# A three-layer graph network on one core: pieces of up to 104 edges in five units, other list lengths, distances on ScalarE, leaky relu on GpSimd

## The chip, the core and the metric

The kernel runs on one core of a Trainium2 chip. The metric is the device time of one execution in microseconds. Its engines work side by side, each through its own queue in order: TensorE (PE in the profile, its weight loads PEld), VectorE (DVE), ScalarE (ACT), GpSimd (POOL) and SyncE (SP, here only for starting transfers). Gathers by an index are started by GpSimd.

## The reference, cut to what matters

```python
def _sage_conv(x, src, dst, Wl, bl, Wr):
    agg = jax.ops.segment_max(x[src], dst, num_segments=x.shape[0])
    agg = jnp.where(jnp.isfinite(agg), agg, 0.0)
    return agg @ Wl + bl + x @ Wr

h = jnp.maximum(_layernorm(x, axis=-1), 0.0)
h = leaky_relu(_sage_conv(h, src, dst, Wl1, bl1, Wr1), 0.01)
h = leaky_relu(_sage_conv(h, src, dst, Wl2, bl2, Wr2), 0.01)
h = leaky_relu(_sage_conv(h, src, dst, Wl3, bl3, Wr3), 0.01)
return x + h
```

There are 6250 nodes and 200000 edges, sorted by destination; the first nodes have by far the most edges. The widths are 128, 256, 256 and 128.

## The kernel before

The nodes are cut into 50 tiles of 127 (the last one shorter). For each destination the maximum over its sources is taken in two ways. For each pair of source tiles g (25 pairs), a product of the rows of that pair with a one-hot matrix picks one source row per destination column, and VectorE takes the maximum into an accumulator. Edges that find their place taken go into lists, whose rows GpSimd gathers from the table of node values, and VectorE takes their maximum too.

Destination tiles are "units" in five groups. Narrow units (24 and 4) have one column per pair of source tiles; middle (11) and wide units (8) have one for each source tile. The three heaviest tiles (`VT`) are cut into pieces of up to `CUT_V` = 96 edges; the pieces fill `NV` = 6 virtual units of 128 rows, and each of these has two columns per source tile: the unit itself and its extra ("x") unit for the second edge. So that group has 12 units in `PLANES`, in parts of 8 and 4. `Joined` puts the pieces of a node together again.

A step is one part of one pair's columns: 8 units in layer 0, up to 4 in layers 1 and 2, so 225, 375 and 375 steps. `products` (L1002) does the matrix products of a step, `maxima` (L1026) the maxima, once for the narrow units and once for each of the two source tiles for the others. One-hots are made by ScalarE (L983, L985) from index bytes, up to six buffers ahead.

The order is written out: `plan(t, rank, f)` enters work for step t, and the main loop runs the ranks of a step in a fixed order (list indices, transposes of h, half of the products, maxima of lists and "chores", rows, rest, linear, merge, gathers, fetches, the other half of the products).

- The lists: `CAPS` gives the length of the list for each block of 128 rows (rows are sorted by length), `PACK` that of one group of rows which are longer still. `Listed.gather` (L1064) gathers one row for each of 128 destinations and writes zeros into a scratch tile after it, 300 columns, as a pause (L1068). `Listed.maximum` (L1079, L1084) follows 4 to 8 steps later. The gathers of a layer are spread over its steps. Eight tiles of gathered rows exist. The index tile of each gather is made by ScalarE (L1053).
- The chores: work on the edge lists that is still to be done during layer 0. `late_rows` sorts and sends lists, `late_lookups` finds for each group of units, in batches of five pairs, which edge belongs to which pair: `expand` (L772) computes the distance of each edge's code to the pair's code by an exclusive or, halves the row by minima (L778) and reduces it (L779); `lookups` transposes the result on TensorE and ScalarE copies it out (L806). The code of a source is its tile times 128, plus its place, plus one, and the lowest bits of the exclusive or are the place if tile and pair agree.
- The nodes: `Node` finishes one tile. Fetch at step ta, merge at ta + 3, `linear` (L1147, L1149; ScalarE copies z to s, L1151) at ta + 4, `rows` at ta + 5 (VectorE's leaky relu into h, L1158, or L1162 in the last layer, and the store of h), `turn` at ta + 6 (TensorE transposes h, L908; ScalarE copies the transpose and h rounded to the product's type, L910 and L913), `rest` in the same step (VectorE's remainder of the rounding, L918, and its store). Nodes come one per step in layer 0 and for the wide units, and one in two steps otherwise in layers 1 and 2.

If a list or a tile does not fit its limits, a flag sends the run through a general path, which redoes all by loops over single edge columns.

## Time and profile before

| | us |
|---|---|
| median of 3 runs (3161.16 to 3170.59) | 3166.22 |
| the profiled execution | 3162.05 |
| its span | 3160.2 |
| VectorE busy | 2717.8 (86%) |
| GpSimd busy | 2430.8 (77%) |
| TensorE busy | 2332.1 (74%) |
| ScalarE busy | 1433.9 (45%) |

Busy shares are means over stretches with different limits. The stretches used further on were found by counting the products of L1002 in program order: layer 0 begins at 229 us, layer 1 at 1216 us, layer 2 at 2201 us, and the span ends at 3160 us. From 397 to 538 us the look-ups of the virtual units are among the chores; from 665 to 825 us the first 24 nodes of layer 0 are finished, one per step; from 1116 to 1284 us the other nodes of layer 0. From 1284 to 1836 us and from 2270 to 2820 us layers 1 and 2 have products and lists alone; from 1836 and from 2820 us on nodes are finished beside them.

### The profile page before, as it was taken

How to read it: one execution, taken by the hardware profiler on the slowest of the kernel's cores; microseconds unless marked ns; L12 is line 12 of the kernel's file. 1: busy time of each engine (PE TensorE's matmuls, PEld its weight loads, DVE VectorE, ACT ScalarE, POOL GpSimd, SP SyncE). 2: the span in 40 equal slices, each digit the busy share in tenths (PEclk: the TensorE clock that was granted, in tenths of full speed). 3: DMA queues.
4: the chain of work that ended last, by engine and by line, in shares of the span. 5: the costliest groups of instructions: out<-in, count | busy, mean ns of one | idle time of the engine just before them, and what ended most of it. 6: DMA issues, size and time to landing. Idle time of an engine off the chain costs nothing.

```text
span 3160.2 us, 37328 instructions
## 1 busy us (share of the span) xinstructions
PE 2332.1 (74%) x9394; PEld 1710.8 (54%) x9394; DVE 2717.8 (86%) x4441; ACT 1433.9 (45%) x2394; POOL 2430.8 (77%) x3424
## 2 busy tenths in 40 slices
PE   1024554456566778899888878889999988888997
PEld 1023333334344455677666656666676666666665
DVE  6668988987898975999999988876799999998995
ACT  5214443333544666555454434444555545443342
POOL 6666888688778883888888786763688888788882
PEclk9996766777767999999999999999999999999998
DMA  9322334266645797556454456778455554555675
GB/s 259 116 65 82 116 111 115 80 179 215 197 156 174 221 270 243 160 157 189 144 153 151 149 162 217 235 217 265 155 172 162 174 141 156 157 153 174 201 221 153
DMA packets 303458, 538.58 MB, mean 170 GB/s; under 512 B 57245, under 2 KB 165589, under 8 KB 302595
## 3 DMA queue, kind: packets, MB, share of 16 engines
q1 hardware_dynamic: 206573, 302.97, 29.7%
q0 software_dynamic: 78592, 196.07, 23.0%
q10 hardware_dynamic: 18070, 37.07, 3.1%
q8 instruction: 79, 1.29, 0.2%
q14 instruction: 144, 1.18, 0.1%
HBM read 409.84 MB, written 126.04 MB: 170 GB/s over the span
## 4 chain that ended last, share of the span: by engine, by line
DVE 19%; PE 16%; POOL 12%; DMA 6%; issue 6%; ACT 1%; SPq 0%; DVEq 0%; POOLq 0%; ACTq 0%
DVE acc L1026 13%; PE pg L1002 11%; POOL g L1064 8%; DMA g<-table,let 4%; POOL gap_t L1068 3%; DVE g L1079 2%; DVE g L1084 2%; PE z_p L1147 2%; PE z_p L1149 1%; DMA out_dram<-s 1%; DMA pair_sb<-pair 1%; ACT hot L985 0%; DMA agg_v<-best,end_i 0%; PE hT_p L908 0%; DMA xt<-in_x_dram 0%
## 5 line engine op out<-in xcount | busy, mean ns | idle before, releaser
L1002 PE MATMUL pg<-hot,pair_sb 128*128 128x512 f32 (+1 forms) x7500 | 2036.3, 421 | 414.2 <-DVE acc L1026 241.3
L1002 PEld LDWEIGHTS pg<-hot,pair_sb 128*128 128x128 f32 x7500 | 1436.1, 202 | 873.4 <-issue 285.9
L1064 POOL DMA_INDIRECT g<-table,let x1518 | 1523.9, 1004 | 492.6 <-issue 237.6
L1026 DVE TENSOR_TENSOR acc<-acc,pg 128x1024 f32<-128x1024 f32 (+4 forms) x1614 | 1663.6, 1057 | 207.1 <-PE pg L1002 164.7
L985 ACT ACTIVATE hot<-idx_sb 128x1024 fp32r<-128x1024 uint8 (+2 forms) x1050 | 909.6, 886 | 714.0 <-PE pg L1002 548.5
L1068 POOL MEMSET gap_t<- 128x300 f32 x1518 | 566.5, 373 | 0.7
L983 ACT ACTIVATE hot<-idx_sb,last_b 128x1024 fp32r<-128x1024 int8 (+1 forms) x300 | 310.3, 1034 | 37.2 <-PE pg L1002 24.9
L1118 POOL DMA_INDIRECT agg<-best,end_i x141 | 140.1, 994 | 104.1 <-PE aT_p L1134 60.5
L1151 ACT COPY s<-z_p 127x256 f32<-127x256 f32 (+1 forms) x150 | 50.4, 336 | 363.2 <-PE z_p L1149 325.8
L1079 DVE TENSOR_TENSOR g<-g 128x1024 f32<-128x1024 f32 (+6 forms) x214 | 207.8, 971 | 0.3
L1084 DVE TENSOR_TENSOR g<-g 128x256 f32<-128x256 f32 (+3 forms) x377 | 183.2, 487 | 11.2 <-issue 0.2
L1147 PE MATMUL z_p<-wr,hT_in 128*128 128x256 f32 (+1 forms) x500 | 138.7, 395 | 0.6 <-DMA hT_in<-across 0.6
L1149 PE MATMUL z_p<-wl,mz 128*128 128x256 f32 (+1 forms) x500 | 121.4, 360 | 11.9 <-DVE mz L1140 11.9
L908 PE MATMUL hT_p<-ident,h 128*128 128x128 f32 x200 | 44.3, 306 | 88.2 <-DVE h L1158 82.0
L973 DVE TENSOR_SCALAR idx_sb<-idx_sb,own_b 128x512 int32<-128x512 int32 (+3 forms) x125 | 73.4, 588 | 35.8 <-DMA idx_sb<-idx 30.6
L910 ACT COPY hT<-hT_p 128x254 f32<-128x254 f32 x100 | 37.1, 371 | 145.8 <-PE hT_p L908 129.0
L1149 PEld LDWEIGHTS z_p<-wl,mz 128*128 128x128 f32 x500 | 89.5, 204 | 25.1 <-DVE mz L1140 14.9
L652 POOL DMA_INDIRECT picks<-picked,to_i x53 | 61.5, 1161 | 48.2 <-DVE rank_f L629 23.5
L1140 DVE TENSOR_TENSOR mz<-acc,aT_p 128x256 f32<-128x256 f32 (+1 forms) x141 | 52.4, 371 | 53.3 <-PE aT_p L1134 53.3
L1147 PEld LDWEIGHTS z_p<-wr,hT_in 128*128 128x128 f32 x500 | 80.7, 203 | 31.7 <-issue 13.3
L908 PEld LDWEIGHTS hT_p<-ident,h 128*128 128x128 f32 x200 | 24.1, 149 | 120.1 <-issue 54.9
L806 ACT CAST v<-lk_p 25x1024 uint8<-25x1024 bf16 (+4 forms) x16 | 11.5, 747 | 165.7 <-PE lk_p L804 165.7
(291 smaller groups left out, 1298.0 us busy)
## 6 DMA issues: line engine op xcount, KB each, us to landing
pair_sb<-pair SPq DMA_DIRECT2D x106, 512.0 KB
idx_sb<-far SPq DMA_DIRECT2D x100, 384.0 KB
pair<-pr SPq DMA_DIRECT2D x100, 256.0 KB
g<-table,let POOLq DMA_INDIRECT x1518
pair_sb<-pair SPq DMA_DIRECT2D x85, 256.0 KB
idx_sb<-idx SPq DMA_DIRECT2D x50, 384.0 KB
far<-idx_sb ACTq DMA_DIRECT2D x50, 384.0 KB
idx_sb<-far SPq DMA_DIRECT2D x50, 352.0 KB
```

The lines of the kernel that those rows point to most:

```text
L973: nc.vector.tensor_scalar(words, words, own_b.bitcast(I32)[:, 0:1], None, op0=OP.bitwise_xor)
L983: nc.scalar.activation(hot[:, :w], far_b.bitcast(I8), AF.Relu, bias=last_b, scale=-1.0)
L985: nc.scalar.activation(hot[:, :w], far_b, AF.Relu, bias=1.0, scale=-1.0)
L1002: nc.tensor.matmul(to, pr[:, s, i, kk * P : (kk + 1) * P], hot[:, o : o + bw], start=((alone or s == 0) and i == 0), stop=((alone or s == ...
L1026: nc.vector.tensor_max(to, to, of)
L1064: nc.gpsimd.indirect_dma_start(out=self.tiles[q, b][:, i, :], out_offset=None, in_=tables[self.layer], in_offset=bass.IndirectOffsetOnAxis ...
L1068: nc.gpsimd.memset(gap_t, 0.0)
L1079: nc.vector.tensor_max(base[:, : i + 1, :], base[:, : i + 1, :], g[:, : i + 1, :])
L1084: nc.vector.tensor_max(base[:, :h, :], base[:, :h, :], base[:, w - h : w, :])
L1118: nc.gpsimd.indirect_dma_start(out=self.agg[:, : self.F], out_offset=None, in_=of, in_offset=bass.IndirectOffsetOnAxis(ap=at, axis=0),)
L1147: nc.tensor.matmul(z_p, self.hT[:, i, :], wr[layer][:, i, :], start=False, stop=False)
L1149: nc.tensor.matmul(z_p, self.m[:, i, :], wl[layer][:, i, :], start=False, stop=(i == K - 1))
```

## The change

- `NV` = 5 and `CUT_V` = 104: the pieces of the three heaviest tiles fill five units. `PLANES` has 10 units there, in parts of 8 and 2.
- `CAPS`: other list lengths; with `PACK`'s 16 they add up to 490 gathers a layer, before 506.
- A source's code is now its tile times 256 (`FAR`), plus its place, plus one. For all but the narrow units `expand` computes the distance as an absolute difference on ScalarE (one bias column per tile, `keys`); the minima are a function of their own (`shrink`), and a batch's distances are issued one batch ahead, into one of four scratch areas. Narrow units and the list's rows are corrected to the old codes by a few short instructions.
- `linear` has two passes of ScalarE over z, relu(z) and relu(-0.01 z), and `rows` subtracts the second from the first on GpSimd (`in_place`); so does `rest` with the remainder of the rounding. Each such subtract lets two later gathers go without their pause (`SPARE`).

```diff
-VT, NV, CUT_V = 3, 6, 96
+VT, NV, CUT_V = 3, 5, 104
 CAPS = (
-    (13, 11, 10, 9, 8, 8, 7, 7, 6, 6, 6, 6, 5, 5, 5, 4, 4, 4, 3, 3, 3, 2, 2, 1),
-    (26, 22, 18, 13, 9, 5),
+    (13, 11, 10, 9, 8, 8, 7, 7, 6, 6, 6, 5, 5, 5, 4, 4, 4, 4, 3, 3, 2, 2, 1, 1),
+    (29, 23, 18, 13, 9),
...
-    (33, 24, 20, 17, 15, 13, 11, 9),
-    (14, 10, 8, 6),
+    (30, 23, 19, 16, 14, 12, 10, 8),
+    (14, 10, 8, 5),
...
+        pick, off = picked[k][:, i0 : i0 + n, :], S(1, I16, n, m)
+        nc.vector.tensor_scalar(pick, top, -float(LEAF), 0.0, op0=OP.add, op1=OP.max)
+        nc.vector.tensor_scalar(off, pick, 1.0 / FAR, -0.499, op0=OP.mult, op1=OP.add)
+        nc.vector.scalar_tensor_tensor(pick, off, -float(FAR - P), pick, op0=OP.mult, op1=OP.add)
...
+            a = 2 * (g0 + i) + s
+            if wide:
+                nc.scalar.activation(t[:, i, :, :], r[:, :, :J], AF.Abs, bias=keys[:, a : a + 1], scale=1.0)
+            else:
+                nc.vector.tensor_scalar(t[:, i, :, :], r[:, :, :J], a * FAR, None, op0=OP.bitwise_xor)
...
+    paused = [0]
+
+    def in_place(out, a, b):
+        nc.gpsimd.tensor_tensor(out, a, b, op=OP.subtract)
+        paused[0] += SPARE
...
-        nc.vector.tensor_sub(pr[:, 1, :F], h[:, :F], pr[:, 0, :F].bitcast(F32))
+        in_place(pr[:, 1, :F], h[:, :F], pr[:, 0, :F].bitcast(F32))
...
-            nc.gpsimd.memset(gap_t, 0.0)
+            if paused[0]:
+                paused[0] -= 1
+            else:
+                nc.gpsimd.memset(gap_t, 0.0)
...
-            nc.scalar.copy(s[:R, :FO], z_p[:R, :])
+            self.h = b = h_ts[turn_h[0] % len(h_ts)]
+            turn_h[0] += 1
+            nc.scalar.activation(s[:R, :FO], z_p[:R, :], AF.Relu)
+            nc.scalar.activation(b[:R, :FO], z_p[:R, :], AF.Relu, scale=-SLOPE)
...
-                nc.vector.scalar_tensor_tensor(h[:R, :FO], s[:R, :FO], SLOPE, s[:R, :FO], op0=OP.mult, op1=OP.max)
+                in_place(h[:R, :FO], s[:R, :FO], h[:R, :FO])
...
-            nc.vector.scalar_tensor_tensor(s[:R, :FO], s[:R, :FO], SLOPE, s[:R, :FO], op0=OP.mult, op1=OP.max)
+            in_place(s[:R, :FO], s[:R, :FO], h[:R, :FO])
...
+                    got[0] = expand(us, J, 0, s, S_acc, next(areas))
+                if g0 + BATCH < NG:
+                    got[g0 + BATCH] = expand(us, J, g0 + BATCH, s, S_acc, next(areas))
+                shrink(got.pop(g0), us, J, g0, got["least"])
```

GpSimd where layer 0 finishes one node per step, before: g are tiles of gathered rows, let their index tiles, agg a node's fetched maximum.

```order
L1064 DMA g_5249<-table0_75,let_5100 128x128
L1068 MEMSET gap_t_891 128x300
L1064 DMA g_5249<-table0_75,let_5206 128x128
L1068 MEMSET gap_t_891 128x300
L1118 DMA agg_5357<-best128_0_140,end_i0_861 128x128
```

The same place of GpSimd's queue in the changed kernel:

```order
L1092 DMA g_4711<-table0_75,let_4609 128x128 x2
L1149 DMA agg_4774<-best128_0_140,end_i0_861 128x128
L941 TENSOR_TENSOR h1_1482<-s_4764,h1_1482 127x256
L941 TENSOR_TENSOR pr_4792<-h0_1481,pr_4792 128x256
L1092 DMA g_4819<-table0_75,let_4672 128x128 x3
L1149 DMA agg_4823<-best128_0_140,end_i0_861 128x128
```

Two subtracts now stand between the fetch of one step and the gathers of the next, and the pauses are gone there. No gather of layer 0 goes without its pause before the first node; 129 of its 490 do, and the first 71 of layer 1 and the first 84 of layer 2.

VectorE at the first look-ups of the virtual units, before (acc is the accumulator's unused half, the scratch area of the chores):

```order
L772 TENSOR_SCALAR acc_1500<-rows_w 128x576 x5
L778 TENSOR_TENSOR acc_1500<-acc_1500 128x30x48
L778 TENSOR_TENSOR acc_1500<-acc_1500 128x30x24
L778 TENSOR_TENSOR acc_1500<-acc_1500 128x30x12
L778 TENSOR_TENSOR acc_1500<-acc_1500 128x30x6
L779 TENSOR_REDUCE least<-acc_1500 128x5x6
L1026 TENSOR_TENSOR acc_1500<-acc_1500,pg 128x1024
```

VectorE there in the changed kernel:

```order
L793 TENSOR_TENSOR acc_1504<-acc_1504 128x25x52
L793 TENSOR_TENSOR acc_1504<-acc_1504 128x25x26
L794 TENSOR_REDUCE least<-acc_1504 128x5x5
L1054 TENSOR_TENSOR acc_1504<-acc_1504,pg 128x1024
L1001 TENSOR_SCALAR idx_sb<-idx_sb,own_b 128x768
```

And ScalarE there in the changed kernel (hot are one-hots, L783 the distances):

```order
L783 ACTIVATE acc_1504<-rows_w,keys 128x520 x10
L1011 ACTIVATE hot<-idx_sb,last_b 128x1024
L1081 ACTIVATE let<-ell_852 128x1
L1013 ACTIVATE hot<-idx_sb 128x1024
L1468 DMA far_158<-idx_sb 128x3072
L783 ACTIVATE acc_1505<-rows_w,keys 128x520 x5
```

The five distances of a batch have left VectorE, which halves twice and reduces; ScalarE has them between its one-hots, two batches at a group's start and then one ahead.

## Rows read from the trace of the kernel before

**Rows 1.** Stretches: length, busy us of PE, PEld, DVE, ACT, POOL; clock, DMA.

```profile
229.00:397.00 168.00, 83.74 (x276) 62.87 (x276) 152.16 (x387) 79.12 (x106) 127.05 (x187) 0.73 0.35 107
397.00:538.00 141.00, 73.25 (x224) 53.37 (x225) 125.50 (x258) 52.12 (x75) 125.88 (x181) 0.68 0.41 114
538.00:665.00 127.00, 55.94 (x181) 39.94 (x180) 117.96 (x290) 45.65 (x69) 95.24 (x137) 0.72 0.36 105
665.00:825.00 160.00, 103.87 (x360) 68.65 (x359) 129.73 (x281) 66.62 (x145) 130.55 (x180) 0.77 0.68 208
825.00:1116.00 291.00, 190.32 (x598) 128.06 (x599) 259.41 (x466) 153.84 (x247) 240.45 (x341) 0.79 0.62 185
1116.00:1284.00 168.00, 142.54 (x570) 97.47 (x569) 114.99 (x202) 106.40 (x198) 99.33 (x138) 0.93 0.79 242
1284.00:1836.00 552.00, 494.80 (x2002) 368.44 (x2003) 525.72 (x568) 276.84 (x403) 480.40 (x705) 0.98 0.51 159
1836.00:2201.00 365.00, 314.56 (x1394) 236.73 (x1393) 289.95 (x366) 150.34 (x309) 237.97 (x323) 0.97 0.70 219
2270.00:2820.00 550.00, 494.06 (x1999) 365.18 (x2000) 522.14 (x559) 276.11 (x400) 474.82 (x701) 0.99 0.52 159
2820.00:3129.00 309.00, 267.02 (x1295) 204.05 (x1294) 277.98 (x366) 115.42 (x220) 234.19 (x318) 0.96 0.66 198
```

**Rows 2.** Groups of VectorE's instructions: busy us, mean ns, idle before, releaser.

```profile
L1026 DVE TENSOR_TENSOR acc<-acc,pg 128x1024 f32<-128x1024 f32 x1096 | 1305.9, 1216 | 149.3 <-PE pg L1002 123.5 <-ACT acc L1024 4.4 <-ACT hot L985 1.3
L1026 DVE TENSOR_TENSOR acc<-acc,pg 128x512 f32<-128x512 f32 x272 | 186.0, 684 | 15.8 <-PE pg L1002 5.6 <-ACT acc L1024 2.5
L1026 DVE TENSOR_TENSOR acc<-acc,pg 128x256 f32<-128x256 f32 x50 | 21.0, 420 | 1.7
...
L1079 DVE TENSOR_TENSOR g<-g 128x1024 f32<-128x1024 f32 (+6 forms) x214 | 207.8, 971 | 0.3
L1158 DVE SCALAR_TENSOR_TENSOR h<-s 127x256 f32<-127x256 f32 x100 | 42.1, 421 | 8.8 <-ACT s L1151 4.9 <-DMA table<-h 3.8
L918 DVE TENSOR_TENSOR pr<-h,pr 128x256 fp32r<-128x256 f32 x100 | 42.0, 420 | 14.0 <-ACT pr L913 13.8
L772 DVE TENSOR_SCALAR acc<-rows_w 128x576 int16<-128x576 int16 (+1 forms) x100 | 38.9, 453 | 0.0
L772 DVE TENSOR_SCALAR acc<-rows_x 128x576 int16<-128x576 int16 x50 | 19.7, 458 | 0.0
L772 DVE TENSOR_SCALAR acc<-rows_m 128x528 int16<-128x528 int16 x50 | 17.6, 417 | 0.0
L1162 DVE SCALAR_TENSOR_TENSOR s<-s 127x128 f32<-127x128 f32 x50 | 14.3, 286 | 6.3 <-ACT s L1151 6.2
```

**Rows 3.** The same view of GpSimd, from 1284 to 1836 us.

```profile
L1064 POOL DMA_INDIRECT g<-table,let x352 | 352.5, 1002 | 71.4 <-issue 52.0 <-ACT let L1053 12.2 <-DVE acc L1026 3.8
L1068 POOL MEMSET gap_t<- 128x300 f32 x353 | 129.2, 366 | 0.2
```

**Rows 4.** Timeline of GpSimd in layer 1: start, us, instruction, idle before.

```profile
1420.46 0.36 POOL L1068 MEMSET gap_t<- 128x300 f32 x1
1420.99 0.95 POOL L1064 DMA_INDIRECT g<-table,let  x1 [0.17 <-issue]
```

**Rows 5.** Timeline of GpSimd in the setup, gathers without pauses.

```profile
63.84 0.94 POOL L400 DMA_INDIRECT rows_n<-cols,at_i  x1 [0.30 <-issue]
```

**Rows 6.** Groups of ScalarE's instructions.

```profile
L985 ACT ACTIVATE hot<-idx_sb 128x512 fp32r<-128x512 uint8 x225 | 140.5, 629 | 132.6 <-PE pg L1002 123.4 <-DVE idx_sb L973 4.8 <-DMA idx_sb<-far 2.3
...
L1151 ACT COPY s<-z_p 127x256 f32<-127x256 f32 x100 | 37.2, 372 | 191.0 <-PE z_p L1149 187.8 <-DMA pair_sb<-pair 1.9 <-DMA hT_in<-across 1.4
```

**Rows 7.** Groups of GpSimd's instructions, its one computing instruction in the setup.

```profile
masks.py:199 POOL TENSOR_SCALAR_AFFINE_SELECT ident<-ident 128x128 f32<-128x128 f32 x1 | 0.3, 292 | 0.1
```

**Rows 8.** Waits from 1840 to 2200 us: us in total, times, longest.

```profile
POOL g L1064 <- ACT let L1053: 66.3, 21, 9.6
...
PE hT_p L908 <- DVE h L1158: 32.6, 29, 4.0
```

More of the change, by code (lines that the diff above doesn't have):

```diff
@@ L44 @@
 P = 128
+FAR = 2 * P
 BIG = 2.0**127
@@ L72 @@
 PAUSE = 300
+SPARE = 2
 @with_exitstack
@@ L92 @@
     widths = (D, H, H)
-    PAST = NG << 8
-    assert NT * P <= PAST and PAST + NT * P < LEAF
+    PAST = NG * 2 * FAR
+    assert NT * FAR <= PAST < LEAF and LEAF + PAST < 1 << 15
     WIDE = list(range(VT, 11))
@@ L109 @@
     EXTRA = [("x", v) for v in range(NV)]
-    PLANES = [units + (EXTRA[4:] + EXTRA[:4] if k == VIRT else []) for k, units in enumerate(GROUPS)]
+    EC = (2 * NV) % 4
+    assert 4 < NV < 8 and 2 * NV - EC == 8
+    PLANES = [units + (EXTRA[EC:] + EXTRA[:EC] if k == VIRT else []) for k, units in enumerate(GROUPS)]
     STARTS = ((0, 40, 25, 53, 60), (0, 10, 0, 19, 28), (0, 10, 0, 19, 28))
@@ L783 @@
     turns = itertools.cycle(("tr", "z"))
+    areas = itertools.cycle(range(4))
+    keys = keep.tile([P, NT], F32, name="keys")
+    nc.vector.tensor_scalar(keys, iota_f[:, :NT], -float(FAR), None, op0=OP.mult)
     stored = [0] * len(GROUPS)
```

38 lines of the change are left out of this document (20 added, 18 removed).

## The prediction

> **What bounds the kernel now.** I read the busy shares first (VectorE is the fullest engine, GpSimd the second), then cut the span into stretches by counting the products of L1002 in program order, and asked of each stretch which engine has no time left in it. The table by stretch answers that [rows 1]. In the long middles of layers 1 and 2 (1284 to 1836 us and 2270 to 2820 us) VectorE is busy 525.7 of 552 us and 522.1 of 550 us. GpSimd shows 480.4 of 552 us, but it is full too: before each of its 352 gathers there it sat idle, 71.4 us in all, 52.0 of it "issue" [rows 3], and 480.4 + 71.4 is the whole stretch. A gather, its pause and the gap before the next gather make 0.95 + 0.36 + 0.17 = 1.48 us [rows 4]. So two engines are full at once there, and a gain on one alone would stop at the other. In layer 0 VectorE is again the fullest (152.2 of 168, 125.5 of 141, 118.0 of 127 us), with GpSimd level with it from 397 to 538 us (125.9 us) and from 665 to 825 us (130.6 of 160) [rows 1]. Where nodes are finished in layer 1 (1836 to 2201 us), TensorE leads: 314.6 of 365 us, and 32.6 us of its idle time are transposes waiting for VectorE's leaky relu [rows 1, 8].
>
> **Fewer units: the heaviest columns.** The last part of the virtual units has two units, not four. In layers 1 and 2 the maxima of that part are 1024 wide, two for each of 25 pairs; they become 512 wide: 50 x (1.216 - 0.684) = 26.6 us of VectorE in each layer [rows 2]. In layer 0 they go from 512 to 256: 50 x (0.684 - 0.420) = 13.2 us. TensorE loses the same columns; it is not the bound there.
>
> **Shorter lists.** 506 gathers a layer become 490 (the lengths and the one group over 96 or 104 edges, added up). I counted the lists from the reference's inputs: 637 pieces for 640 rows, and no list is longer than its new limit. GpSimd saves 16 x 1.48 = 23.7 us a layer, of which 11 gathers, 16 us, lie in the middle. VectorE saves the maxima of 16 gathered rows, some 0.3 us each in layers 1 and 2 (a 1024-wide maximum over four of them takes what L1026 takes): 5 us.
>
> **Subtracts on GpSimd.** VectorE loses L1158, L918 and L1162: 42.1 + 42.0 + 14.3 = 98.4 us [rows 2]. ScalarE gets a second pass over each z, 0.37 us [rows 6], 150 times; it has time, and the path from z to h grows by that much. GpSimd gets 250 subtracts. No row shows one of two inputs. Below, VectorE's 0.42 us bounds it [rows 2]; above, GpSimd's own select, with one input, took 0.29 us for 128 columns [rows 7], so 512 columns read take at most 1.2 us. A pause writes 300 columns in 0.36 us [rows 4]; at its rate 512 take 0.62 us, and I take 0.65, with 0.42 to 1.2 us for the range (at 1.2 the 38 nodes that meet a full GpSimd, below, cost 40 us more). Against that, each subtract drops two pauses. A dropped pause does not give back its 0.36 us: gathers that follow each other directly stand 0.30 us apart [rows 5] instead of 0.36 + 0.17, so it gives 0.24 us. A node with two subtracts costs GpSimd 1.3 us and gives back 0.95 us.
>
> Where the credit is spent matters more: by the order of the changed kernel the first 71 gathers of layer 1 and the first 84 of layer 2 run without a pause, since the nodes of the layer before left that many. About 55 and 75 of them lie in the middles: 13 and 18 us off GpSimd, just where it was full.
>
> The Trainium skill, "GPSIMD Engine Reference", section "Elementwise — side-by-side cycle accounting", puts a two-input add at about twice VectorE's time and advises VectorE for such work, which speaks against this move; from its 4497 ns for 2048 columns 256 columns would be 0.56 us (an estimate), and by it the 250 subtracts would be 22 us shorter in all than by my 0.65. The trace does not show such an instruction; rows 1 show why the advice need not hold here, VectorE being the engine without time.
>
> **Order on GpSimd.** The price of the move is that GpSimd's queue now waits. A subtract of "rows" waits for ScalarE's two passes, one of "rest" for ScalarE's rounding, and behind each stand the gathers and fetches of that step and all later ones. Before, GpSimd ran some steps ahead in these stretches, held only by the index tiles. A gather has 4 to 8 steps until its maximum, and a fetch 3 until its merge, so the loss of the lead is covered where GpSimd has slack (238 of 365 us busy in layer 1's nodes [rows 1]). It is not covered where it has none. From 665 to 825 us one node is finished per step: 24 nodes x 0.35 = 8 us more on GpSimd against 4 us fewer gathers; with its gaps it was nearly full, so it sets the pace and only about 9 us come off, though VectorE loses over 35. From 1116 to 1284 us some 14 nodes come one per step beside gathers, and I count 5 us of loss.
>
> **Distances on ScalarE.** 200 instructions leave VectorE: 38.9 + 19.7 + 17.6 = 76.2 us [rows 2]. On ScalarE 512 to 528 elements cost about 0.63 us, by the one-hot of 512 [rows 6]; 200 x 0.63 = 126 us. The hundred of the virtual units fall mostly into 397 to 538 us, where ScalarE was busy 52.1 of 141 us [rows 1]: 52 + 63 = 115 us, which fits. But ScalarE is in order. The first two batches of each group stand behind the copy that waits for the last batch's result, so VectorE waits some microseconds at each of eight group starts. With GpSimd full as well I take 15 us of some 35 us that leave this stretch. On 104 columns two halvings and a reduction over 26 take the place of four halvings and one over 6, which I count as even. The added corrections in the pick (20 short instructions) and in the setup cost some 10 us of VectorE, of which I put 3 on the path.
>
> **The sum.** Middles of layers 1 and 2: VectorE loses 26.6 + 5 = 31.6 us, GpSimd 16 + 13 or 16 + 18; both bounds fall by about 30, and I take 27 each, 54. Layer 0: 0 (229 to 397), 15 (to 538), 4 (to 665, where the distances of the middle tiles begin), 9 (to 825), 14 (to 1116: half of L772's 38.9 us and 7 us of narrower maxima leave VectorE, while GpSimd loses 14), and -5 (to 1284): 37. Layer 1's nodes: h comes from an engine with time, which I let remove 20 of the 32.6 us of waits [rows 8]. Layer 2's nodes (VectorE 278.0 of 309 us [rows 1]): 14.3 us leave it and the sum of two tiles must now wait for GpSimd; 10. Setup and the last nodes: -3. Together 54 + 37 + 20 + 10 - 3 = 118 us. The profiled execution took 3162 us (its span 3160.2); 3162 - 118 = 3044, and against the median of 3166.2, 3048. I predict 3046.
>
> **Rivals.** (a) The relief passes through: GpSimd's lead and its spent credit suffice, and VectorE stays the only bound. It loses about 76 + 98 + 66 + 12 = 252 us; of these 42 in layer 1's nodes lie beside TensorE. The other 210 would give about 2955. Against it: GpSimd full in rows 1 and 3.
> (b) Only the narrower columns and shorter lists pay; what is moved off VectorE is lost again in waits of the two in-order queues. Then 54 + 13 + about 8 us come off: 3090.
> (c) Subtracts and gathered maxima collide. If a VectorE instruction on two SBUF tiles held up a subtract or was held up by it, the 207.8 us of L1079 [rows 2] and as much again at L1084, an eighth of the time, would meet some 30 to 60 of 250 subtracts, at up to 1.2 us: 25 to 50 us back, 3070 to 3095. The pauses were writes only, so rows cannot show it. The Trainium skill, "SBUF — State Buffer", section "Who interferes with whom", states just this: such a VectorE instruction contends with a GpSimd one that reads SBUF, not with one that only writes.
> (d) Slower: GpSimd's queue blocks. Each of the 150 nodes holds the gathers behind its subtract, as waits for index tiles held them 66.3 us in 21 times, 3.2 us each [rows 8]. If the maxima wait for those gathers, 37 nodes eat the gain (118 / 3.2); half the nodes would give 3166 + 122 = 3288 us. For it: 24 nodes at one per step in layer 0. Against it: the 4 to 8 steps between a gather and its maximum, 3.6 us each in layer 1's nodes (365 us for 100 steps).
> (e) The change doesn't do what it says: a list over its limit sends the run through the general path, many times longer. By the count above, hardly.
>
> **How the numbers follow.** Forecast 0.55 (3000 to 3070), (a) 0.13, (b) 0.14, (c) 0.10, (d) 0.04, (e) 0.01, and 0.03 for no change. The range runs from half way to (a) to beyond (b) and (c): 2980 to 3110, which leaves out most of (a), and (d), (e) and no change. About 0.3%, 10 us, is what a measurement of this kernel tells from no change. Faster by more: 0.92; within: 0.03; slower: 0.05.
>
> **What would show it.** VectorE's busy time some 250 us lower, GpSimd's some 85 us lower; the middles at about 525 us each, both engines still full; no wait of VectorE for gathered rows. Subtracts of 0.5 to 0.8 us. The transposes of h waiting under 15 us in layer 1. Wrong it is if VectorE waits for ScalarE's distances by more than some 30 us, if gathers stand behind subtracts with maxima waiting, or if the middles did not shorten.

## The result and the profile after

| | us |
|---|---|
| before, median of the runs beside it | 3165.2 (3161.2 to 3170.6) |
| after, median | 3118.9 (3106.8 to 3125.3) |
| ratio | 0.9848 [0.9813, 0.9883] |
| profiled execution of after | 3125.3, its span 3123.5 |

The change gains 46 us, not the 118 of the sum, and lies 9 us above the range. The line of busy time of the whole span, from the page of after (before: VectorE 2717.8, GpSimd 2430.8):

```profile
PE 2311.0 (74%) x9374; PEld 1706.8 (55%) x9374; DVE 2506.6 (80%) x3932; ACT 1553.8 (50%) x2723; POOL 2351.3 (75%) x3096
```

VectorE lost 211 us of work (I had said 250), GpSimd 80 (I had said 85). The work went where it was to go; the time did not follow. To see where, the starts of the steps are read from the products, counted in program order, for both profiled executions (steps are numbered through all three layers; these two executions differ by 37 us, the medians by 46):

```
stretch (steps)              before   after   difference   predicted
layer 0, 0 to 58              308.8   283.6      -25          -15
layer 0, 58 to 225            678.0   660.2      -18          -22
layer 1 starts, 225 to 250     68.1    72.9       +5            0
layer 1 middle, 250 to 500    551.5   564.5      +13          -27
layer 1 nodes, 500 to 600     365.5   335.2      -30          -20
layer 2 starts, 600 to 650    123.0   130.5       +8 (with the middle)
layer 2 middle, 650 to 875    496.1   509.6      +14          -27
layer 2 nodes, 875 to 974     308.4   299.1       -9          -10
tail                           31.5    38.5       +7           (+3 with the setup)
```

Layer 0 and layer 1's nodes did a little better than forecast, layer 2's nodes as forecast. The two middles, with 54 of the 118 us, went the other way. The rows of after that answer to [rows 1] (length, busy us of PE, PEld, DVE, ACT, POOL; granted clock, DMA): the start of layer 1, its middle, its nodes, layer 2's middle and nodes.

```profile
1173.00:1246.00 73.00, 61.79 (x267) 45.21 (x267) 32.52 (x42) 47.20 (x88) 40.17 (x47) 0.95 0.63 197
1246.00:1811.00 565.00, 492.33 (x2002) 369.93 (x2003) 500.13 (x555) 267.78 (x400) 443.21 (x629) 0.96 0.48 148
1811.00:2146.00 335.00, 310.70 (x1392) 237.28 (x1392) 263.60 (x285) 160.82 (x350) 252.24 (x279) 0.97 0.76 239
2217.00:2786.00 569.00, 493.30 (x2001) 370.74 (x2002) 496.38 (x548) 266.49 (x397) 434.48 (x613) 0.96 0.47 146
2786.00:3085.00 299.00, 263.32 (x1289) 199.71 (x1287) 267.09 (x325) 121.12 (x258) 221.68 (x273) 0.97 0.68 204
```

In layer 1's middle VectorE fell from 525.7 to 500.1 us and GpSimd from 480.4 to 443.2, close to the sum's terms, and the stretch grew from 552 to 565. TensorE stayed at 492 us although a sixth of the virtual units' columns is gone, at a mean clock of 0.96 where it was 0.98. The waits of that middle in after (us in total, times, longest), and then two of before:

```profile
POOL g L1092 <- ACT let L1081: 63.3, 25, 8.0
PE pg L1030 <- DVE acc L1054: 57.7, 80, 3.3
...
DVE acc L1054 <- PE pg L1030: 51.2, 58, 3.2
```

```profile
PE pg L1002 <- DVE acc L1026: 45.7, 61, 2.9
...
DVE acc L1026 <- PE pg L1002: 11.1, 18, 1.9
```

TensorE waits for VectorE's maxima (57.7 us; before 45.7) and VectorE waits for TensorE's products (51.2 us; before 11.1). GpSimd waits for ScalarE's index tiles, which stand behind one-hots that wait for TensorE. No engine is full any more, and the stretch is longer.

The mean time of a step by its place, from its first product to the next step's, over both middles, says where (columns 16 to 20 of the narrow tiles are units 16 to 19 of that group; granted clock: mean over the same steps):

```
                                      us              granted clock
step                                 before   after   before   after
virtual units, first step             2.53     2.51    0.98     0.97
virtual units, second step            2.71     2.76    0.98     0.97
virtual units, third (512 -> 256)     2.46     2.45    1.00     0.97
narrow tiles, columns 16 to 20        1.90     2.52    1.00     0.85
narrow tiles, columns 20 to 24        1.87     1.99    1.00     0.95
```

The first and second of these steps follow each other; steps of other groups stand between the second and the third.

The step that was made half as wide lasts as long as before, and the one right after it, with nothing changed in it, takes 0.62 us more. One such place in the timeline of after, TensorE and then VectorE (start, us, instruction, idle before), and the windows of the same place:

```profile
1356.66 2.20 PE L1030 MATMUL pg<-hot,pair_sb 128*128 128x512 f32 x9
1359.40 0.71 PE L1030 MATMUL pg<-hot,pair_sb 128*128 128x256 f32 x4 [0.54 <-DVE acc L1054]
1360.54 0.71 PE L1030 MATMUL pg<-hot,pair_sb 128*128 128x256 f32 x4 [0.42 <-DVE acc L1054]
1361.67 5.69 PE L1030 MATMUL pg<-hot,pair_sb 128*128 128x512 f32 x17 [0.42 <-DVE acc L1054]
```

```profile
1357.86 5.05 DVE L1054 TENSOR_TENSOR acc<-acc,pg 128x256 f32<-128x256 f32 x6
1365.26 1.22 DVE L1054 TENSOR_TENSOR acc<-acc,pg 128x1024 f32<-128x1024 f32 x1 [2.35 <-PE pg L1030]
```

```profile
1359.40:1361.70 2.30, 1.45 (x9) 1.10 (x9) 2.30 (x3) 2.16 (x3) 2.07 (x4) 1.00 0.96 296
1361.70:1365.00 3.30, 3.30 (x8) 2.54 (x9) 1.10 (x2) 0.88 (x3) 2.08 (x3) 0.53 0.40 144
```

The short products are done in 0.71 us and wait 0.42 to 0.54 us for a buffer each time, because VectorE is still at maxima of earlier steps. Then TensorE's granted clock is at 0.53, about its lower level (1.2 of 2.4 GHz), for the next step: eight products in 3.30 us. By then VectorE has caught up and stands still for 2.35 us. What it was relieved of, it spends waiting.

### The profile page after: what moved, and what is told of

Read it like the earlier page. It is cut to its first block, busy times and chain, and to the rows that moved or that the text cites. A ratio compares the mean times of both kernels' runs of the same rounds, so it can differ in the third digit from the quotient of the medians.

```text
span 3123.5 us, 36856 instructions
## 1 busy us (share of the span) xinstructions
PE 2311.0 (74%) x9374; PEld 1706.8 (55%) x9374; DVE 2506.6 (80%) x3932; ACT 1553.8 (50%) x2723; POOL 2351.3 (75%) x3096
## 5 line engine op out<-in xcount | busy, mean ns | idle before, releaser
L1030 PE MATMUL pg<-hot,pair_sb 128*128 128x512 f32 (+2 forms) x7500 | 2020.3, 418 | 447.8 <-DVE acc L1054 237.3
L1054 DVE TENSOR_TENSOR acc<-acc,pg 128x1024 f32<-128x1024 f32 (+4 forms) x1614 | 1600.5, 1016 | 327.4 <-PE pg L1030 287.7
L1092 POOL DMA_INDIRECT g<-table,let x1470 | 1468.9, 999 | 483.0 <-issue 257.8
L1013 ACT ACTIVATE hot<-idx_sb 128x1024 fp32r<-128x1024 uint8 (+3 forms) x1050 | 877.8, 856 | 720.2 <-PE pg L1030 519.0
L1099 POOL MEMSET gap_t<- 128x300 f32 x994 | 371.6, 374 | 0.5
L1115 DVE TENSOR_TENSOR g<-g 128x256 f32<-128x256 f32 (+2 forms) x363 | 188.7, 520 | 17.9 <-DMA g<-table,let 7.6
L941 POOL TENSOR_TENSOR h<-s,h 127x256 f32<-127x256 f32 x100 | 75.1, 751 | 41.3 <-ACT h L1185 34.5
L1001 DVE TENSOR_SCALAR idx_sb<-idx_sb,own_b 128x512 int32<-128x512 int32 (+4 forms) x125 | 76.4, 611 | 36.2 <-DMA idx_sb<-idx 33.3
L941 POOL TENSOR_TENSOR pr<-h,pr 128x256 fp32r<-128x256 f32 x100 | 76.9, 769 | 35.9 <-ACT pr L935 33.4
L930 PE MATMUL hT_p<-ident,h 128*128 128x128 f32 x200 | 43.4, 301 | 72.4 <-POOL h L941 56.9
L793 DVE TENSOR_TENSOR acc<-acc 128x1300 int16<-128x1300 int16 (+6 forms) x110 | 68.1, 619 | 25.4 <-ACT acc L783 23.1
```

Of the source, the lines that this page charges most:

```text
L941: nc.gpsimd.tensor_tensor(out, a, b, op=OP.subtract)
L1013: nc.scalar.activation(hot[:, :w], far_b, AF.Relu, bias=1.0, scale=-1.0)
L1030: nc.tensor.matmul(to, pr[:, s, i, kk * P : (kk + 1) * P], hot[:, o : o + bw], start=((alone or s == 0) and i == 0), stop=((alone or s == ...
L1054: nc.vector.tensor_max(to, to, of)
L1092: nc.gpsimd.indirect_dma_start(out=self.tiles[q, b][:, i, :], out_offset=None, in_=tables[self.layer], in_offset=bass.IndirectOffsetOnAxis ...
L1099: nc.gpsimd.memset(gap_t, 0.0)
```

## Experiments

Every ratio below is to the kernel before in runs on the same chip. These runs were on four chips on which both kernels are slower than in the first result (before 3205 to 3234 us). One of the four ran the variants with parts undone, one the changed kernel again with three variants, one the cleared credit and the two reliefs, one the three cuts at the end. A comparison across chips is weaker: in the six traces whose middles have the changed kernel's steps unaltered (after, undo_leaky, undo_dist, keep_pauses, changed_again, clear_credit), layer 1's middle takes 563 to 575 us and layer 2's 506 to 514. Differences of a few us between middles therefore say little.

**One part undone at a time.** First the pieces:

```
-VT, NV, CUT_V = 3, 5, 104        +VT, NV, CUT_V = 3, 6, 96
-    (29, 23, 18, 13, 9),         +    (26, 22, 18, 13, 9, 5),
-EC = (2 * NV) % 4                +EC = 4
```

> The changed kernel with the pieces alone undone: six units of up to 96 edges again, so that the last step of the virtual units is 512 columns wide as before; lists, distances and subtracts stay as changed. Theory N (narrow step): in the middles of layers 1 and 2 the 256-wide step of the virtual units lasts as long as the 512-wide one did (2.35 and 2.63 us against 2.43 and 2.52), and the step right after it, columns 16 to 20 of the narrow tiles, rose from 1.90 and 1.96 to 2.49 and 2.68 us, with TensorE waiting for VectorE and its granted clock at the lower level there. Then the middles, 564.5 and 568.9 us in the changed kernel, come back to 552 or less, 535 to 552 each, with under 25 us at the lower clock in each, though VectorE has 26 us more to do: 3085 to 3105 in all. Rival G (GpSimd: dropped pauses and subtracts are what slows the middles) and rival S (subtracts or gathers collide with VectorE's maxima): the wide columns come on top, the middles 570 to 590, 3140 to 3170 in all.

Measured: 0.9994 [0.9968, 1.0020], 3207 us. The middles (layer 1, and layer 2 from step 650):

```profile
1327.00:1881.00 554.00, 493.43 (x1999) 365.84 (x2000) 519.77 (x555) 276.62 (x399) 438.55 (x624) 0.98 0.50 153
2364.00:2862.00 498.00, 444.73 (x1805) 329.69 (x1804) 469.68 (x500) 249.95 (x362) 403.42 (x579) 0.99 0.51 151
```

10 and 12 us shorter than in after (14 and 17 against changed_again below), with 20 us more work on VectorE and the clock back at 0.98 and 0.99: the pieces are what lengthened the middles. The total missed theory N's number by 100 us. Most of that is the chip: the changed kernel itself took 3197 us on one of the later ones. Beside that kernel, layer 0 lost 19 us (978 and 959 us for its 225 steps), for one virtual unit more costs chores too, and the setup took 17 us more (262 and 244 us); why, the runs don't show. And GpSimd has 42 us less to do than in [rows 1], VectorE 6, and the middle is as long as before: GpSimd did not bind it.

Then the leaky relu and the rounding's rest, back on VectorE:

```
-nc.scalar.activation(s, z_p, AF.Relu); nc.scalar.activation(b, z_p, AF.Relu, scale=-SLOPE)
+nc.scalar.copy(s, z_p)
-in_place(h, s, h)          +nc.vector.scalar_tensor_tensor(h, s, SLOPE, s, op0=OP.mult, op1=OP.max)
-in_place(pr[:, 1], h, pr[:, 0])    +nc.vector.tensor_sub(pr[:, 1], h, pr[:, 0])
...      (slices left out; the last layer likewise)
```

> The changed kernel with leaky relu and the rounding's rest back on VectorE; no subtract on GpSimd, so every pause is kept too. Theory N: the middles stay at 564 to 570 us each; layer 1's nodes go back from 335 to about 365 us, layer 2's from 299 to about 308, layer 0 gives back 10 to 20: 3165 to 3180 in all, slower than the kernel before or level with it. Rival G or S: the middles fall to some 525 to 545 us, and the total stays at 3100 to 3140.

Measured: 0.9873 [0.9835, 0.9911], 3166 us. The middles stay, 563.1 and 514.2 us, without one subtract or dropped pause in the kernel, so rivals G and S fall. Layer 1's middle:

```profile
1251.00:1814.00 563.00, 488.33 (x1998) 366.62 (x1999) 499.54 (x555) 268.08 (x401) 472.77 (x686) 0.96 0.49 150
```

The nodes go back to 366.8 and 315.2 us, as expected within about 7 us. What was not expected: the total is better than the changed kernel's (0.9973, below, on another chip), since the starts of the layers are 66.8 and 125.7 us and layer 0 takes 940 us, 20 less.

> The changed kernel with the distances of all tiles on VectorE again. All theories: layers 1 and 2 as in the changed kernel, middles 562 to 571 us. Layer 0: 76 us return to VectorE; by the prediction's sum the distances brought 15 us (397 to 538 us of the span), a few of the next stretch, and most of the 14 us from 825 to 1116, so layer 0 ends 20 to 30 us later than the changed kernel's 1173: 3138 to 3150 in all. If ScalarE's distances had cost waits as large as their relief, the total would stay at 3119.

(`if wide:` in `expand` replaced by `if False:`.) Measured: 1.0005 [0.9977, 1.0032]. The total, expected at 3138 to 3150 us, is 3209 on this slower chip. Layer 0's 225 steps take 975 us, against 959 in the changed kernel on another chip: the distances on ScalarE bring some 15 us, where 20 to 30 were expected. Layer 1's middle is 574.6 us, the longest of the six, though nothing was changed in it.

> The changed kernel with every pause between gathers kept (a subtract earns no dropped pause). Theory N: the middles do not move, 560 to 572 us each; the starts of layers 1 and 2 (72.9 and 130.5 us in the changed kernel, 68.1 and 122.9 before) may come back by up to 5 and 8 us, the nodes lose some; 3110 to 3135 in all. Rival G: gathers that follow each other without a pause crowd the transfers and hold up VectorE; with the pauses the middles fall to 525 to 545 us and the total to 3060 to 3090.

(`SPARE = 0`.) Measured: 0.9956 [0.9937, 0.9975], 3191 us; middles 567.3 and 510.0, unmoved, though GpSimd has 474 us of work in layer 1's for 438 with dropped pauses; starts 70.7 and 130.9 us, where undo_dist, with the credit and on the same chip, has 81.5 and 140.4.

This run and undo_leaky say most about the subtracts: they ran on the same chip, every pause is kept in both, and the one difference is whether leaky relu and the rounding's rest are on GpSimd or on VectorE. The kernel with them on GpSimd is the slower one, 3191 and 3166 us. In steps 75 to 108, where layer 0 finishes one node per step, this run and then undo_leaky have (fourth busy time: ScalarE; fifth: GpSimd):

```profile
630.00:834.00 204.00, 121.24 (x423) 82.42 (x422) 122.03 (x223) 118.36 (x258) 184.17 (x255) 0.73 0.64 187
```

```profile
629.00:809.00 180.00, 113.50 (x423) 78.97 (x422) 128.51 (x269) 110.27 (x232) 156.13 (x215) 0.77 0.72 211
```

GpSimd is busy 184 of 204 us there, and 24 us are lost. The starts lose 4 and 5 us. In layer 1's nodes the move brings 15 us (352.2 for 366.8), and the dropped pauses bring 17 more (334.9 in undo_dist). Transposes waiting for h in layer 1's nodes, in undo_leaky and then in keep_pauses:

```profile
PE hT_p L930 <- DVE h L1189: 34.0, 29, 2.6
```

```profile
PE hT_p L930 <- POOL h L941: 20.3, 23, 1.6
```

**The changed kernel and three variants.** The base:

> The changed kernel itself, beside its variants on one chip: the base against which the next three are read. All theories: 0.98 to 0.99 of the kernel before; 250 steps of layer 1's middle in 560 to 572 us.

Measured: 0.9973 [0.9947, 0.9999], 3197 us. On this chip the change is worth some 9 us (the ratio; the medians differ by 12), and it misses the 0.98 to 0.99 that were expected. Its starts of layers 1 and 2 take 84.0 and 140.3 us, not 72.9 and 130.5; the middles, 568.7 and 514.1, are within 5 us of the first chip's:

```profile
1287.00:1856.00 569.00, 489.07 (x2000) 366.93 (x2001) 500.28 (x556) 267.89 (x401) 438.09 (x623) 0.96 0.48 146
...
2332.00:2846.00 514.00, 446.15 (x1801) 333.56 (x1800) 451.05 (x497) 242.44 (x362) 399.56 (x578) 0.95 0.47 144
```

The timeline at the start of layer 1, VectorE and GpSimd:

```profile
1258.91 0.69 DVE L1054 TENSOR_TENSOR acc<-acc,pg 128x512 f32<-128x512 f32 x1 [3.66 <-issue]
1265.21 0.69 DVE L1054 TENSOR_TENSOR acc<-acc,pg 128x512 f32<-128x512 f32 x1 [5.62 <-remote]
1271.62 3.48 DVE L1054 TENSOR_TENSOR acc<-acc,pg 128x1024 f32<-128x1024 f32 x3 [5.72 <-remote]
```

```profile
1263.67 0.95 POOL L1092 DMA_INDIRECT g<-table,let  x1 [0.30 <-issue]
1264.92 0.94 POOL L1092 DMA_INDIRECT g<-table,let  x1 [0.30 <-issue]
1266.17 0.95 POOL L1092 DMA_INDIRECT g<-table,let  x1 [0.30 <-issue]
1267.42 0.95 POOL L1092 DMA_INDIRECT g<-table,let  x1 [0.30 <-issue]
```

While GpSimd issues one gather after the other with no pause between, VectorE stands still for 5.6 and 5.7 us, released by nothing that the profile can name ("remote"); ScalarE shows 5.25 and 5.33 us at the same times, and TensorE waits for VectorE. The first chip's trace of the same kernel has no such wait.

The products of the narrow step made twice, to 512 columns:

```
+again = [to] if K == 1 or bw > 256 else [to, p[:, kk, 256 : 256 + bw]]
+for to in again:
     for i in range(2): nc.tensor.matmul(to, ...)
```

> The changed kernel, where in layers 1 and 2 the products of the 256-wide step are made twice, the second time into a part of PSUM that nothing reads: TensorE streams 512 columns there as before, VectorE's maxima stay 512 wide (256 by two). Theory N1 (the clock: TensorE, done early, waits there and its granted clock falls): time at the lower clock in a middle falls from 37 to 48 us to 25 or less, the step after the narrow one from 2.5 to 1.9 to 2.1 us, and the middles to 545 to 556 us, 10 to 20 us less each, though TensorE has 0.96 us more to do for each pair. Theory N2 (the narrow step's time is VectorE's: lists' maxima are spread by steps, as many of them on the narrow step as on a wide one, and products and maxima hand the same three buffers to and fro): more products can't help, middles 562 to 590 us.

Measured: 0.9886 [0.9861, 0.9911], 3177 us, clear of the changed kernel's 3197 on the same chip. The middles:

```profile
1289.00:1851.00 562.00, 497.26 (x2166) 382.37 (x2165) 498.14 (x553) 267.35 (x399) 443.36 (x624) 0.97 0.48 148
2327.00:2831.00 504.00, 448.46 (x1952) 342.59 (x1951) 450.55 (x497) 242.90 (x362) 402.45 (x576) 0.98 0.48 146
```

By the steps they are 562.9 and 504.3 us, 6 and 10 less. The step after the narrow one takes 2.15 us instead of 2.52, at a mean granted clock of 0.96 instead of 0.85; the narrow one takes 2.80 instead of 2.55. More work on TensorE made the kernel faster. So the clock is part of it; the 6 and 10 us are short of the 10 to 20 that N1 said, and of the 27 that were missing. The 6 alone would lie within what such middles vary by; the total and the step do not.

Steps of 4, 3 and 3 units, and the narrow step with fewer gathered rows:

```
-EC = (2 * NV) % 4      +EC = 3
+size = 2 * NV - EC if k == VIRT else HOT // P      (parts of 7 and 3 units, not 8 and 2)
```

> The changed kernel with the ten virtual rows of columns cut into steps of 4, 3 and 3 units (512, 384 and 384 columns) rather than 4, 4 and 2; the same columns in all, and one maximum more that covers two kinds of unit. Theory N1: no step is short enough for TensorE to run far ahead; the clock stays up, middles 535 to 552 us. Theory N2: VectorE's work is spread more evenly over the steps: middles 540 to 558 us. If neither (the maxima's sum is what counts), the middles stay at 560 to 572.

Measured: 0.9837 [0.9806, 0.9868], 3162 us; middles 557.0 and 500.2, 12 and 14 us less, at the upper end of N2's range and outside N1's.

> The changed kernel, where the planner gives the 256-wide step of layers 1 and 2 a weight of 0.4 in place of 1.25, so that about a third as many gathered rows fall on it; the products and maxima of columns are untouched. Theory N2: the narrow step falls from 2.45 to about 1.6 to 1.9 us, the others rise by less in sum; middles 540 to 555 us. Theory N1: the narrow step gets shorter for VectorE as for TensorE, the clock may hold: also 540 to 558, with less than 25 us at the lower clock. If the lists' maxima do not matter: 560 to 572.

Measured: 0.9911 [0.9882, 0.9941]; middles 550.4 and 498.1, but the nodes 7 and 11 us longer, since the rows moved there. The narrow step itself stayed at 2.49 us: a miss. So its own gathered rows are not what makes it long; VectorE's backlog from the steps ahead would explain it, but no run tests that.

**The same relief at two places.** This decides between place and sum. With six units and all products, half of the maxima of one step is left out, in one kernel of the first of three steps, in the other of the third:

```
+if layer and k == VIRT and c == 0 and g != first_g[layer, k]:     (c == 8 in the other)
+    of, to = of[:, :, : 2 * P], to[:, :, : 2 * P]
```

> The kernel with pieces undone (six units, 512 columns in each of the three steps of the virtual units, middles 554 and 497 us counted from step 650), where in layers 1 and 2 the maxima of the first of these steps are left out for half of its columns (two of four units); all products stay. VectorE loses 25 x 2 x 0.53 = 26.6 us in each middle, as much as the change took off it, but in the first step of the three. Theory P (place: what counts is whether VectorE or TensorE is behind just there): here VectorE is behind for two wide steps in a row, so the relief passes through at least in half: middles 530 to 543. Rival Q (it is the sum: TensorE and VectorE are coupled by three buffers, and no relief of VectorE shortens the middle any more): 548 to 556.

Measured: 0.9813 [0.9759, 0.9867], 3174 us.

```profile
1312.00:1846.00 534.00, 483.22 (x2000) 365.25 (x2001) 496.87 (x555) 276.42 (x400) 435.22 (x622) 0.99 0.52 158
2325.00:2807.00 482.00, 436.96 (x1801) 329.64 (x1800) 449.29 (x499) 249.72 (x362) 403.01 (x575) 0.99 0.52 156
```

> The same kernel with pieces undone, where the half of the maxima is left out of the third step of the virtual units, the one which the change narrowed; all products stay at 512 columns. Theory P: the relief falls just ahead of steps in which TensorE is the slower one, and little passes through: middles 548 to 556. Theory N1 (the narrow products and the clock are all that spoiled it): 528 to 540, since the products are wide here. Rival Q: 548 to 556, and relief_first the same.

Measured: 0.9922 [0.9901, 0.9942], 3211 us.

```profile
1326.00:1880.00 554.00, 496.22 (x2000) 368.50 (x2000) 498.20 (x555) 276.13 (x399) 439.25 (x622) 0.98 0.50 152
2360.00:2855.00 495.00, 442.96 (x1804) 328.13 (x1803) 450.78 (x500) 249.74 (x362) 399.51 (x577) 0.99 0.51 152
```

The third busy time is VectorE's: 496.9 and 498.2 us in layer 1's middle, against 519.8 with nothing left out. From the first step, 20 of the 23 us pass through (554 to 534); from the third, none (554 to 554). In layer 2 it is 16 and 3 us. Both ran on one chip, and their totals are 37 us apart. Theory P holds; the sum on VectorE says little.

**The credit.** 

```
+if any(b <= t < b + 16 for b in begins):
+    paused[0] = 0
```

> The changed kernel, where the credit of dropped pauses is set to zero during the first 16 steps of each layer: a layer's first gathers have their pauses again, later ones still lose two for each subtract. Theory C (instructions arrive late where gathers run without pauses: on the two chips seen since, the traces of the changed kernel show VectorE and ScalarE waiting some 30 and 50 us for no engine and no transfer of the kernel, above all around 830, 1185, 1270 and 2250 us, against 3 and 12 us with every pause kept): on such a chip the starts of layers 1 and 2 fall from 84 and 140 to about 71 and 131 us, the nodes stay at 335 and 308 us, 3165 to 3185 us where the changed kernel took 3197 and the kernel before 3205 to 3210; on a chip like the first one the starts fall from 73 and 130.5 to 69 and 124. Rival: the starts are long because subtracts and ScalarE's second pass delay the last nodes; then nothing moves by more than 5 us.

Measured: 0.9821 [0.9780, 0.9862], 3176 us; the starts of layers 1 and 2:

```profile
1217.00:1288.00 71.00, 60.32 (x267) 44.42 (x265) 31.97 (x41) 46.57 (x86) 43.01 (x61) 0.98 0.62 199
2188.00:2319.00 131.00, 113.46 (x482) 87.39 (x481) 83.11 (x98) 70.48 (x117) 99.07 (x142) 0.95 0.53 166
```

13 and 9 us less than 84.0 and 140.3, and 12 to 14 and 11 to 12 less than in the two reliefs on this chip, which keep the credit but have six units (83.5 and 85.1, 141.5 and 143.2); the rival said under 5. The nodes keep 335.4 us in layer 1. The ratio shows more than this mend: against the changed kernel the time is 21 us less, 0.7%, and the rest of the step from 0.9973 to 0.9821 is that the kernel before was slower on this chip. VectorE's unnamed waits in front of L1054, over the whole span, changed kernel and then this one (us, times, longest; "issue" too is time in which it waited for nothing that the profile shows):

```profile
DVE acc L1054 <- issue: 72.4, 62, 6.6
DVE acc L1054 <- remote: 46.1, 13, 7.7
```

```profile
DVE acc L1054 <- issue: 68.9, 76, 6.5
...
DVE acc L1054 <- remote: 19.3, 4, 8.4
```

The first kind hardly falls. With every pause kept it is 43.6 us (keep_pauses) and 49.0 (undo_leaky) on these chips, and the first chip's trace of the changed kernel has neither kind before L1054.

Both mends together:

> The changed kernel with both mends, steps of 4, 3 and 3 units and the credit cleared at a layer's start; a version that may beat both. If the two add: 0.985 of the changed kernel or less, 3135 to 3150 us on a chip where the kernel before takes 3207, 3065 to 3095 on the first chip; middles 550 to 558 us, starts 69 to 72 and 124 to 131. If the one undoes the other (more pauses make GpSimd late in the middles), 3155 to 3170.

Measured: 0.9708 [0.9673, 0.9743], 3142 us where before took 3234. They add: the middles are 554.7 and 497.3 us, near those of even_steps, the starts 72.0 and 124.3, near or under those of clear_credit (71.5 and 130.8).

**Place without leaving anything out.** Three cuts of the same ten units, same maxima and products in sum; the credit is cleared in all.

> The version with steps of 4, 3 and 3 units and the credit cleared, once more, as the base for the next two on one chip: 0.965 to 0.975 of the kernel before, 250 steps of layer 1's middle in 552 to 558 us, steps 650 to 875 in 495 to 502.

Measured: 0.9732 [0.9696, 0.9767], 3129 us; middles 551.4 and 500.0.

```
-for c in range(c0, c0 + pw // P, n // P): ...
+cuts = list(range(c0, c0 + pw // P, n // P))
+if k == VIRT and n < pw:
+    cuts[1] = c0 + 3      (2 in split_244; EC = 4, parts of 6 and 4)
...
```

> The same with the ten units cut into steps of 3, 3 and 4: the two narrow steps come first and the wide one last. The maxima of a pair sum to the same 3.27 us for each plane on VectorE, and TensorE's columns are the same; the place alone differs. Theory P (a relief of VectorE passes through where VectorE is behind and stays behind, as where it was left out of the first step: 534 and 482 us): the middles fall to 535 to 548 and 482 to 494 us, 10 to 15 us less each than with 4, 3 and 3. Rival Q (only the sum counts): within 4 us of it.

Measured: 0.9713 [0.9678, 0.9749], 3117 us. The middles:

```profile
1273.00:1816.00 543.00, 480.61 (x2004) 370.64 (x2003) 498.98 (x556) 267.88 (x399) 466.77 (x685) 0.97 0.51 155
2271.00:2756.00 485.00, 427.31 (x1801) 328.59 (x1800) 449.26 (x497) 241.69 (x362) 412.91 (x606) 0.98 0.51 153
```

> The same with steps of 2, 4 and 4 units: the changed kernel's narrow step, put first of the three instead of last. Same sums on VectorE and TensorE as in the changed kernel and in the 4, 3, 3 version. Theory P: the 256-wide step now stands ahead of a wide one, so VectorE's relief is used up there: middles 533 to 548 and 480 to 494 us. Theory N1 (a 256-wide step costs TensorE its clock wherever it stands): as the changed kernel's, 560 to 570 and 506 to 514, with 40 us at the lower clock.

Measured: 0.9687 [0.9660, 0.9715], 3111 us. The totals of these three have overlapping intervals; their middles tell more.

```profile
1271.00:1819.00 548.00, 485.43 (x2002) 375.79 (x2001) 498.43 (x555) 267.26 (x399) 470.34 (x685) 0.94 0.50 153
2274.00:2760.00 486.00, 427.01 (x1806) 330.37 (x1805) 450.26 (x498) 241.84 (x362) 412.17 (x608) 0.97 0.51 154
```

The kernel to set beside these is clear_credit, which has the same columns in steps of 4, 4 and 2 and the credit cleared; it ran on another chip, but steps of 4, 3 and 3 agree between those two chips within 3 us in each middle (554.7 and 551.4, 497.3 and 500.0). Its middles:

```profile
1288.00:1852.00 564.00, 490.77 (x1999) 368.41 (x1999) 499.38 (x555) 268.41 (x401) 472.88 (x684) 0.96 0.49 149
2319.00:2825.00 506.00, 438.36 (x1800) 328.02 (x1799) 450.51 (x496) 242.37 (x362) 406.60 (x595) 0.97 0.48 145
```

The 256-wide step put first leaves middles of 548 and 486 us, where put last it leaves 564 and 506. This is so although layer 1's mean clock is the lowest of all, 0.94. The clock falls behind the narrow step here too, to 0.85 in the mean of the step after it; but that one is a wide step of the virtual units, where VectorE is the slower engine, and it costs little. Steps of 3, 3 and 4 give 543 and 485. VectorE is busy 498 to 500 us in layer 1's middle in every one of these kernels and in the changed one; their middles reach from 543 to 569 us. 2, 4, 4 with the credit cleared has the lowest ratio of all that ran, 0.969 of the kernel before, though its interval overlaps those of 3, 3, 4 and of 4, 3, 3. The changed kernel did not run on that chip, and none of these versions on the first one.

## Why the prediction was wrong, point by point

- **The middles, -54 forecast, +27 measured: the step that failed.** "Both bounds fall by about 30, and I take 27 each" rests on reading VectorE and GpSimd as full. For GpSimd the reading proved nothing: "480.4 + 71.4 is the whole stretch" adds an engine's busy and idle time, which always make up the stretch. It was not a bound: 42 us less of its work moved nothing (undo_pieces), nor did the pauses (keep_pauses). And VectorE's 525.7 of 552 us is a mean over steps in which now VectorE, now TensorE is behind, with three product buffers between them. TensorE's 494.8 of 552 stands in the same row of [rows 1], and I passed it by with "it is not the bound there". The change took VectorE's relief at the last virtual step, just ahead of steps where TensorE is the slower one: the step of the narrow tiles takes 1.90 us in before, about what its eight products take (nine take 2.20 us at the full clock in the timeline above), for one maximum of 1.22 us [rows 2] and some lists. There it becomes waiting, as relief_third shows, and relief_first and the two splits show that the same relief passes through elsewhere.
- **That alone gives zero, not +13.** "TensorE loses the same columns" was costed at nothing. The shorter products bring TensorE to a halt in front of its buffers, and it is granted half its clock more often (mean 0.96 for 0.98): by the traces' clock 85 us of the two middles, 31 in before. Working at half rate for 55 us longer costs at most 27 us, as much as the two middles grew (an estimate from these two numbers, for steps in which TensorE is the slower engine). Making the products twice took 34 us off the lower clock and gave back 6 and 10 us. What is left, some 9 us a middle against relief_third, the runs don't tell apart.
- **Layer 0, -37 forecast, -43 measured: the sum is right, its terms are not, which is in part luck.** Pieces were costed in layer 0 by their narrower maxima alone, but a unit fewer is a sixth fewer chores for the virtual units: of the 19 us that undoing the pieces costs layer 0, 12 lie in its first 58 steps. The distances brought about 15 us, less than put down. One took 0.71 us on ScalarE, not 0.63. The subtracts cost layer 0 26 us with all pauses kept, on a later chip (keep_pauses 965 us, undo_leaky 940). That GpSimd sets the pace where one node is finished per step was forecast, and rightly; that the move is a loss there was not. What it did to layer 0 on the first chip, no run shows.
- **Layer 1's nodes, -20 forecast, -30 measured, layer 2's -10 and -9: half of the mechanism.** The transposes of h no longer wait for VectorE, as said. But that alone brought 15 us in layer 1; the other 17 came from the dropped pauses, which the prediction had put into the middles: the last 116 gathers of layer 1 go without one, and GpSimd comes to its subtracts sooner. In the nodes of layer 1 in after:

```profile
PE hT_p L930 <- POOL h L941: 5.9, 7, 1.4
```

  5.9 us for the 32.6 of [rows 8], and for the 20.3 of keep_pauses; under 15 was asked.
- **The subtracts**: 0.65 us taken, 0.77 and 0.75 measured for 256 columns (of L941, from the view of GpSimd's groups):

```profile
L941 POOL TENSOR_TENSOR pr<-h,pr 128x256 fp32r<-128x256 f32 x100 | 76.9, 769 | 35.9 <-ACT pr L935 33.4 <-PE z_p L1176 1.8
L941 POOL TENSOR_TENSOR h<-s,h 127x256 f32<-127x256 f32 x100 | 75.1, 751 | 41.3 <-ACT h L1185 34.5 <-DMA hT_in<-across 2.7 <-DMA across<-hT 2.4
```

  The estimate from the figure in the Trainium skill, "GPSIMD Engine Reference", section "Elementwise — side-by-side cycle accounting", was 0.56. Its advice to leave such work on VectorE came out right with all pauses kept, on one chip: 0.9873 [0.9835, 0.9911] on VectorE, 0.9956 [0.9937, 0.9975] on GpSimd. With the pauses dropped except at the layers' starts, the subtracts have 0.9821 [0.9780, 0.9862] on another chip (clear_credit), and which is better then is open.
- **The credit, taken as 13 to 18 us off GpSimd in each middle**: worth nothing there, worth 17 us in layer 1's nodes, and it costs 11 to 14 and 9 to 12 us at the starts of layers 1 and 2 on the later chips. On the first chip the starts are 5 and 8 us longer than in before; that the credit did it is not shown, for with no pause dropped the subtracts alone lengthen them by 4 and 5 (keep_pauses against undo_leaky). That gathers without pauses could hold up other engines stood in no rival.
- **Rivals.** (c) is not what was lost: the 1024-wide maximum of gathered rows takes 1237 ns for 1221, and the middles, where the loss lies, are as long without any subtract. (b) had layers 1 and 2 upside down: the narrower columns are what did not pay there, and the work moved off VectorE did, in the nodes. (d) did not come as said, in layer 1's nodes VectorE does not wait for gathers; but GpSimd's queue did cost time in layer 0. (a) needed a VectorE that is the only bound, and in the middles it is not. (e) did not come. The prediction's own sign of being wrong was that the middles did not shorten.
- **The tail, +7**: 37 to 40 us in every variant that was run, 31.5 before. Some 5.6 us of it lie behind the last computing instruction: from there to the end are 14.9 us in after, 9.3 in before, and 14.5 to 15.6 in every variant, and GpSimd's closing drain takes 7.7 us for 3.4. What makes the drain longer, no run shows.

## What to carry to other kernels

An engine that is busy 95% of a stretch need not be its bound if another one is at 90% and a few buffers lie between them: ask of each step which of the two is behind, and take work off where it is behind and stays so for the next steps. The same 23 us were worth 20 in one step and 0 in another of the same loop. A step that is made shorter on the engine that isn't late there only makes that engine wait. And a change of three parts wants each part priced alone: here the part that moved work to GpSimd lost more in layer 0 (26 us) than it won in the nodes (15 and 4), as long as every pause was kept.

## What the runs showed of the hardware

- On the later chips, and not on the first, VectorE and ScalarE stood still for 5 to 6 us at a time, and TensorE behind them, while GpSimd issued gathers every 1.25 us with no pause. Taking the pauses away is what brings the long stops at the starts of layers 1 and 2: with them the starts are 11 to 14 and 9 to 12 us shorter, seen on two chips (keep_pauses beside undo_dist, clear_credit beside the two reliefs). The "remote" waits before L1054 are 46.1 us with dropped pauses, none (keep_pauses) or 8.0 us (undo_leaky) with all kept; those called "issue" remain, 43.6 and 49.0 us for 72.4. While the long stops last, VectorE is released by nothing named, and in one of the two shown a packet of the queue for instructions moved among 209 of gathers. The Trainium skill, "Runtime: NRT & Kernel Launch", section "Instruction fetch mechanics", says that instructions come by DMA in blocks and that this is mostly hidden; that it is what stops the engines here is a guess that no run tested.
- One and the same changed kernel took 3119 us on one chip and 3197 on another, the kernel before 3165 and 3210: the change gained 46 us on the one and 12 on the other.
- More products on TensorE shortened the kernel (3177 for 3197 us): the step after them took 2.15 us for 2.52, at a mean granted clock of 0.96 for 0.85.
